# Products of B and C on the two halves of rows, and quarters first: one change to a graph-and-Mamba kernel

## The chip, the cores and the metric

The kernel runs on one core of a Trainium2 chip. The metric is the device time of one execution in microseconds (us). Before the change it is 2470.87 us, the median of 14 runs that lie between 2467.94 and 2473.18.

Engines are named as in the profile: PE is TensorE's matmul, PEld its weight load, DVE is VectorE, ACT is ScalarE, POOL is GpSimd, SP is SyncE. "SPq" is the queue in which SP issues transfers. "L744" is line 744 of the kernel before.

## The reference, cut to what matters

The input x is 64 graphs of 256 nodes with 256 features, all in float32, and adj is one 256x256 matrix of zeros and ones for each graph. There are two layers, each with a mixing part and a part like a feed-forward; every part works on a layernorm of x and is added to x.

```python
x = x + graph_attention(layernorm(x), adj)           # per graph, scores masked by adj
x = x + mamba2_block(layernorm(x))                   # d_state 64, 8 heads of 64, conv of 4, chunk 256
x = x + relational_gnn(layernorm(x), relation=adj)   # adj's entries name the relation
x = x + moe_top1(layernorm(x))                       # 8 experts 256 -> 1024 -> 256, capacity 1.25 T/E
```

In the Mamba2 block, a projection, a causal convolution and silu give xh (8 heads of 64), B and C (64 wide each) for every node. With one chunk per graph, the output is

```python
Y_diag = einsum('bcln,bcsn,bhcls,bcshp->bclhp', Cc, Bc, Lmat, xdt)
```

so each graph needs one 256x256 product of C and B, contracted over only 64 values, of which the causal part (s not after l) is used. It is multiplied by each head's decay (Lmat), and the result multiplies that head's xdt. In the last part each node goes to one of 8 experts; nodes past an expert's capacity are dropped.

## The kernel before, in words

**Prologue.** Weights are loaded and folded (the products of two weight matrices, centred weights) in a pool of its own. Its last lines (L586 to L591) transpose the experts' b1 and write it to a scratch tensor, b1d, from which pass 2 reads; that write is issued by SP. Behind it in SP's queue stand the loads of the first group's adj and x (L805 and L803).

**Pass 1** works on 32 groups of two graphs (512 nodes). A group goes through attention (a graph's nodes on partitions in two tiles), `scan`, `mix`, `relate` and `choose`, and writes its x to x3d and out, and each node's expert and place to a table of slots. Nothing loops at run time. Each operation is registered as a step with an engine, a planned duration, what it reads and what it writes; a planner (`Plan.record`, L180 to L290) then emits all steps of all groups in the order in which its own model says that they can begin. Of the steps on one engine that could begin within 0.05 us of each other, the one of lower rank goes first; the rank is `PACE * group + DUE[k]` for the k-th step of a group, and `LATE[k]` for the steps behind the last group. These tables are numbers in the file. The emitted order is kept, so every engine's queue holds the groups interleaved.

**B and C.** In `scan`, the fifth column block of the convolved projection (`convolved(NCT)`) holds B in rows 0 to 63 and C in rows 64 to 127, with the 512 nodes of the two graphs along the columns (`bm`, L969 to L974). A matmul contracts over rows, so B and C have to stand on the same rows: a transfer (L975) copies rows 64 to 127 of `bm` to rows 0 to 63 of `cm`. The other 64 rows of the two buffers of `cm` are set to zero once, in the prologue (L606 to L610), and the products contract over all 128 rows: B's rows meet C, C's rows meet zeros. `meet` (L1059) makes two products for each graph, 256 wide for the first 128 values of s and 128 wide for the second; DVE multiplies each graph's by the causal mask `trif` (L1064) into `bc`. For each pair of heads DVE multiplies the decays `dm` by `bc` (L1088), and `heads` (L1090) multiplies by xdt. The heads' matmuls use half of the array's columns each (64 outputs), two heads in turns; their form in the profile is 128\*64.

**The end of pass 1.** The lists of blocks are made by a long chain of small DVE steps (`walk`, L635 to L655). A block is up to 512 slots of one expert. Two whole blocks (NEARLY = 2) of the experts run as planned steps within pass 1 (`first_block`, L1379 to L1402), beside the last groups.

**Pass 2** (L1480 to L1622) does the other blocks, in three kinds: quarters (128 slots), halves (256) and wholes (512), in this order. Each kind is a nest of run-time conditions, `experts(i)` within `If(listed > i)`. In this run 4 quarters, 1 half and otherwise wholes are done. For a block, `fetch_slots` (SP) loads the table's rows, `gather` (POOL) computes places and fetches the rows of x3d with one indirect transfer for each 128, `fetch_weights` (SP) loads w1, b1, w2 and b2 (1 MB for each of w1 and w2), `norm` (DVE, L415) and `turned` (PE and ACT, L1545) make the block's normed rows and transpose them, `experts` multiplies by w1 (L1563) and w2 (L1573), and the result is scattered to the output (L427). `experts(i)` begins by issuing the weights of block i+1, the slots and the rows of block i+2, and norms block i+1. The second weight buffer of the quarters is also that of the wholes.

Before the loops, the code issues for all three kinds, in this order: the slots of blocks 0 and 1, the rows of blocks 0 and 1, the weights of block 0, and the norm and transposes of block 0. A small matmul then makes a number (`general`) that says whether the program must run again in a general form; it doesn't here. Tile's scheduler puts in the waits; each engine runs its own instructions in the order of the code.

Of the kernel before, what the change touches and what calls it, by code (L numbers as in the profile page):

```python
# [9 lines left out]
F32 = mybir.dt.float32  # L10
# [4 lines left out]
ALU = mybir.AluOpType  # L15
# [4 lines left out]
P = 128  # L20
# [11 lines left out]
PACE = 4.60  # L32
DUE = [
    -187, -691, -72, 159, -113, -114, -149, 636, 174, 171, 387, 756, -229, -1087, -1172, 20, -351,
    -599, 699, -611, -1484, 249, -770, -710, -1048, 376, -331, 864, -405, 61, -28, 134, 16, -9,
    348, 442, -429, -1102, -42, 703, -223, 113, -607, 108, 990, 202, 295, 646, 26, 263, -92, 233,
    247, -557, -374, -723, 667, 329, -360, -253, -391, -1223, -304, -600, -778, -988, -488, -62,
    -720, -720, -306, -566, -4, 261, -344, 153, -232, -603, -36, -391, 947, 502, -439, -94, -126,
    29, -246, 327, -208, -945, 61, -486, -490, -648, -49, 120, 553, 10, -408, -1120, -935, -301,
    -1702, 164, -515, 586, -50, -355, 132, 744, -80, 96, -1, 160, -115, 422, 133, 217, -609, 128,  # L40
    -1196, 106, -198, -115, -589, -56, 549, -876, -729, 476, -280, -741, -486, -186, -114, 171,
    711, -911, -300, -262, 1079, -444, -107, -98, 127, 135, -372, -12, -97, 504, 638, 342, -669,
    -318, 1, 363, -806, -1604, -646, -790, 276, -140, 264, -165, 370, 251, 14, -435, -518, -133,
    -470, -615, 98, 237, -148, -214, -868, -1044, -884, 125, 722, 505, 627, 310, 101, 280, 264,
    947, 409, -79, 138, -8, -1018, -924, -303, -515, -328, -216, -660, 755, 133, 127, -181, 129,
    -683, -19, 86, -697, 353, 242, -391, 243, -479, -626, 320, 328, 221, -542, -377, 191, 161,
    -181, 223, -433, -295, 139, 127, 151, -181, 152, -496, -30, 178, -458, 330, 615, -10, 301,
    198, -168, 566, 303, -1378, -203, 504, -349, 138, 15, 93, -300, -469, -71, -1080, -905, -382,
    -765, -499, 522, -559, -436, -711, -1062, -307, -489, 705, -263, 262, 48, 538, -87, -172, -7,
    -532, -975, -688, -187, -1308, -570, 302, -1059, -506, 779, 83, -11, 749, -4, 216, 469, 900,  # L50
    -1142, 86,
]
LATE = [
    439, 482, 387, 262, 460, 193, 260, 587, 397, 193, 239, 309, 207, 431, 312, 489, 501, 247, 320,
    397, 398, 341, 500, 377, 575, 532, 367, 505, 283, 139, 276, 464, 345, 243, 455, 107, 575, 200,
    296, 296, 296, 296, 296, 296, 296, 296, 296, 296, 296, 296, 170, 321, 356, 486, 13, 179, 363,
    192, 357, 768, 395, 1857, 2047, 1812, 2046, 1886, 2036, 1982, 2016, 1957, 1976, 1757, 1937,
    1678, 2042, 1873, 2052, 2162, 2018, 2061, 1964, 2122, 1809, 397, 1880, 2090, 446, 466, 2153,
    1801, 208, 1845, 1887, 420, 371, 1753, 2084, 343, 1955, 1982, 469, 302, 1752, 1929, 128, 2080,
    1921, 332, 270, 332, 389, 145, 449, 139, 514, 497, 334, 177, 408, 502, 1660, 1834, 1843, 1988,  # L60
    2202, 2247, 2273, 2186, 2179, 1985, 1853, 1933, 1944, 2220, 1882, 2133, 1815, 2009, 2179,
    2095, 1789, 1828, 563, 1802, 1733, -146, 109, 1792, 2073, 414, 1763, 1943, 143, 509, 2344,
    2010, 508, 2033, 2085, 250, 423, 2196, 2256, 716, 2018, 1585, 411, 176,
]


class Home:

# [219 lines left out]
def gnn_mamba_rgcn_moe(ctx: ExitStack, tc: tile.TileContext, a: dict, out: bass.AP):  # L288
# [1174 lines left out]
    def second_pass(form, pass2):  # L1463
# [136 lines left out]
        for blocks in three:  # L1600
            for i in range(2):
                blocks.fetch_slots(i)
# [68 lines left out]
```

## Time and profile before

| What | Value |
|---|---|
| median of 14 runs | 2470.87 us (2467.94 to 2473.18) |
| the profiled execution's own time | 2472.09 us |
| its span in the profile | 2470.4 us |
| PE busy | 2355.6 us (95%) |
| DVE busy | 1915.2 us (78%) |
| ACT busy | 1634.9 us (66%) |
| POOL busy | 825.9 us (33%) |
| PE's last instruction of pass 1 ends | 1846.65 us |
| last result of pass 1 is sent (L427) | 1852.71 us |
| first matmul of pass 2's first quarter begins | 1874.99 us |
| first matmul of its first whole block begins | 1934.31 us |

The profile comes from one execution; its times run from the span's start. A row of a timeline gives the begin, the length from the first begin to the last end of a run of like instructions, the engine, the line, the operation, the tiles (written <- read), the shapes, the count, and in brackets the idle time of the engine before it with what ended it. In a row of stretches, each engine has its busy time with its number of instructions. L744 is the line of a helper, `product`, that many steps use, so its rows are told apart by their tiles. The times in pass 1 that the prediction uses are from the stretch 800 to 1100 us, which is one of steady work.

### The profile page before, as it was taken

The numbers are of one execution on the slowest core, as the hardware profiler recorded it, in microseconds if no ns is written. First come the engines' busy times: TensorE is split into PE (matmuls) and PEld (weight loads), VectorE is DVE, ScalarE is ACT, GpSimd is POOL, SyncE is SP. The second block draws the span as 40 slices with busy tenths as digits, with TensorE's granted clock in tenths as the row PEclk, the third lists the DMA queues.
The fourth block names the chain that finished last, engine by engine and source line by source line (L and its number), as shares of the span: only waits on it lengthen the run. The fifth ranks groups of instructions, "written<-read, shape, count | busy, mean of one in ns | idle before, by whom it ended". The sixth has DMA issues, their size and how long they took to land.

```text
span 2470.4 us, 35015 instructions
## 1 busy us (share of the span) xinstructions
PE 2355.6 (95%) x11448; PEld 1645.7 (67%) x11451; DVE 1915.2 (78%) x4825; ACT 1634.9 (66%) x3720; POOL 825.9 (33%) x762
## 2 busy tenths in 40 slices
PE   5999999999999999999999999999886999999996
PEld 4567777667767666776766777666655566666664
DVE  4899999999999999999999999999772234444333
ACT  2878888888888888888888888887522232223321
POOL 1122334333342433334333343432524222222221
PEclk8999999999999999999999999999997999999998
DMA  3212222322222322222332222321537333333332
GB/s 116 46 23 54 63 62 66 80 57 55 63 62 65 79 59 55 63 55 72 73 65 55 63 55 72 65 55 40 140 106 255 109 115 123 109 111 130 110 116 61
DMA packets 173527, 198.93 MB, mean 81 GB/s; under 512 B 25448, under 2 KB 157870, under 8 KB 173312
## 3 DMA queue, kind: packets, MB, share of 16 engines
q1 hardware_dynamic: 124816, 135.70, 16.8%
q0 software_dynamic: 46816, 58.88, 13.0%
q8 instruction: 98, 1.61, 0.3%
q10 hardware_dynamic: 1680, 1.79, 0.3%
q14 instruction: 117, 0.96, 0.1%
HBM read 112.47 MB, written 45.45 MB: 64 GB/s over the span
## 4 chain that ended last, share of the span: by engine, by line
issue 33%; DVE 33%; POOL 13%; PE 10%; ACT 8%; DMA 3%; POOLq 0%; SPq 0%; ACTq 0%; DVEq 0%
PE ps L744 8%; DVE y L963 8%; POOL rs L752 5%; POOL out_dram L427 3%; POOL xg L409 3%; DVE gate L946 3%; DVE xh L1105 2%; DVE gate L1108 2%; DVE st L760 2%; DVE dm L1088 2%; DMA xg<-x3d,place 2%; DVE xdt L1078 1%; DVE ev L857 1%; DVE ev L859 1%; DVE bm L973 1%
## 5 line engine op out<-in xcount | busy, mean ns | idle before, releaser
L744 PE MATMUL ps<-xnT,win 128*128 128x512 f32 x1152 | 543.4, 601 | 4.0 <-ACT xnT L786 3.9
L963 DVE SCALAR_TENSOR_TENSOR y<-ps,cw,y 128x510 f32<-128x510 f32 (+2 forms) x480 | 351.0, 738 | 6.1 <-ACT y L956 4.5
L752 POOL TENSOR_TENSOR rs<-ve,mhalf 128x4 f32<-128x4 f32 x96 | 161.2, 1679 | 529.5 <-DVE ve L750 405.7
L1030 ACT ACTIVATE dm<-ps,cs 128x256 f32<-128x256 f32 (+1 forms) x1024 | 332.6, 472 | 5.5 <-PE ps L744 5.5
L744 PEld LDWEIGHTS ps<-xnT,win 128*128 128x128 f32 x1152 | 205.0, 190 | 171.0 <-issue 159.7
L1563 PE MATMUL ps<-xnT,w 128*128 128x512 f32 (+2 forms) x736 | 279.2, 539 | 11.2 <-DVEq L1619 6.1
L1573 PE MATMUL ps<-w,hid 128*128 128x256 f32 x1248 | 276.3, 379 | 0.0
L1573 PEld LDWEIGHTS ps<-w,hid 128*128 128x128 f32 x1248 | 235.3, 190 | 38.7 <-issue 8.6
L744 PE MATMUL ps<-wf,gate 128*128 128x265 f32 x1024 | 252.2, 389 | 0.0
L1563 PEld LDWEIGHTS ps<-xnT,w 128*128 128x128 f32 x736 | 134.1, 197 | 146.0 <-issue 138.0
L1088 DVE TENSOR_TENSOR dm<-dm,bc 128x1536 f32<-128x1536 f32 x128 | 225.7, 1764 | 0.5 <-ACT dm L1036 0.2
L1567 ACT ACTIVATE hid<-ps,b 128x512 f32<-128x512 f32 (+2 forms) x184 | 114.5, 622 | 165.0 <-PE ps L1563 163.1
L744 PEld LDWEIGHTS ps<-wf,gate 128*128 128x128 f32 x1024 | 191.7, 190 | 47.9 <-issue 10.9
L1578 DVE TENSOR_TENSOR yv<-ps,b 128x256 f32<-128x256 f32 x78 | 33.1, 425 | 228.4 <-PE ps L1573 228.3
L1036 ACT ACTIVATE dm<-dm 128x1536 f32<-128x1536 f32 x128 | 198.6, 1554 | 0.0
L1282 POOL DMA_INDIRECT slots<-meta,sl x128 | 127.9, 999 | 200.1 <-DVE sl L1279 149.1
L427 POOL DMA_INDIRECT out_dram<-yf,place x78 | 77.7, 997 | 315.5 <-DVE yf L1586 315.2
L1095 PE MATMUL ps<-dm,xdt 128*64 128x256 f32 x1024 | 167.6, 394 | 2.0 <-DVE dm L1088 1.5
L760 DVE BATCH_NORM_STATS2 st<-x 128x6 f32<-128x256 f32 x384 | 151.6, 413 | 6.8 <-DMA x<-in_x_dram 6.2
L969 ACT ACTIVATE xh<-y 128x512 f32<-128x512 f32 x160 | 101.0, 631 | 75.9 <-DVE y L963 66.4
L1579 ACT ACTIVATE yv<-yv,meta 128x256 f32<-128x256 f32 x78 | 39.7, 509 | 168.1 <-DVE yv L1578 168.1
L744 PE MATMUL ps<-wh,eT 128*128 128x273 f32 x512 | 141.7, 406 | 4.6 <-ACT eT L882 4.6
(314 smaller groups left out, 5011.4 us busy)
## 6 DMA issues: line engine op xcount, KB each, us to landing
w<-in_L_ffn_w_dram SPq DMA_DIRECT2D x52, 1024.0 KB, 5.6
x<-blin POOLq DMA_DIRECT2D x32, 530.0 KB, 6.2
x<-brel POOLq DMA_DIRECT2D x32, 530.0 KB, 6.7
adji<-in_adj_dram SPq DMA_DIRECT2D x32, 512.0 KB, 3.8
x<-in_x_dram SPq DMA_DIRECT2D x32, 512.0 KB, 4.7
x3d<-x SPq DMA_DIRECT2D x32, 512.0 KB, 3.1
out_dram<-x SPq DMA_DIRECT2D x32, 512.0 KB, 4.1
cm<-bm SPq DMA_DIRECT2D x32, 128.0 KB, 2.2
```

What stands on the lines that cost most here:

```text
L427: apart("out", nc.gpsimd.indirect_dma_start(out=outf, out_offset=bass.IndirectOffsetOnAxis(ap=col, axis=0), in_=yf, in_offset=None, bounds ...
L744: nc.tensor.matmul(out_, lhsT=lhsT, rhs=rhs, start=(i == 0), stop=(i == len(pairs) - 1))
L752: s.step(POOL, 1.0, lambda: nc.gpsimd.tensor_tensor(rs(), ve(), mhalf[:, 0:4], ALU.pow), [ve], [rs])
L760: s.step(DVE, 0.34, lambda j=j: nc.vector.bn_stats(sb()[:, j, :], src()[:, j, 0:D]), [(src, j)], [(sb, j)])
L963: nc.vector.scalar_tensor_tensor(y3[:, :, d:], p3[:, :, : N - d], cw[:, c, k : k + 1], y3[:, :, d:], ALU.mult, ALU.add,)
L1030: nc.scalar.activation(dm()[:, q, bi, o : o + n], ps()[:, t0 + N - n : t0 + N], AF.Relu, bias=cs()[:, j, h : h + 1], scale=-1.0,)
L1036: s.step(ACT, 1.38, lambda: nc.scalar.activation(dm(), dm(), AF.Exp, scale=-1.0), [], [dm])
L1088: s.step(DVE, 1.67, lambda dm=dm: nc.vector.tensor_mul(dm(), dm(), bc().unsqueeze(1).to_broadcast([P, 2, 2, N + P])), [bc], [dm])
L1095: nc.tensor.matmul(o, lhsT=xdt()[:, 2 * bi, h * 64 : (h + 1) * 64], rhs=dm()[:, q, bi, 0:N], start=True, stop=False,)
L1282: s.step(POOL, 1.1, lambda j=j: apart("slots", nc.gpsimd.indirect_dma_start(out=slots, out_offset=bass.IndirectOffsetOnAxis(ap=sl()[:, j : ...
L1563: nc.tensor.matmul(ps[:, :n], lhsT=w1[:, k, f * P : (f + 1) * P], rhs=xnT[:, k, :], start=(k == 0), stop=(k == 1),)
L1573: nc.tensor.matmul(ps[:, :D], lhsT=hid[:, f, j * P : (j + 1) * P], rhs=w2[:, f, :], start=(f == 0), stop=(f == NFT - 1),)
```

## The change

Three parts of the code change, and the planner's tables.

1. Two transfers of 64 rows by 256 columns take the place of one of 64 rows by 512: C of the first graph goes to rows 0 to 63 of `cm`, and B of the second graph goes to rows 64 to 127 of `cm`. So the first graph's B (`bm`) and C (`cm`) stand on rows 0 to 63, and the second graph's B (`cm`) and C (`bm`) on rows 64 to 127. The products contract over 64 rows, and the two graphs' products are emitted in turns, as one step with two PSUM tiles: the 256 wide ones of both, then the 128 wide ones of both. Nothing has to be zero any more, so the two memsets go.
2. The write of b1d is issued on POOL's queue in place of SP's.
3. Before pass 2's loops, the slots of block 0 of all kinds are loaded, then, for each kind, the rows of block 0 are gathered and the slots of block 1 loaded; then the weights of block 0 are issued; then only the quarters' block 0 is normed and transposed; then the rows of block 1 of all kinds are gathered. The halves' block 0 is normed and transposed behind the quarters' loop, the wholes' behind the halves' loop, and the matmul for `general` comes behind the quarters' loop.
4. PACE, DUE and LATE hold other numbers. DUE has one entry less, since a group has one step less.

```diff
-PACE = 4.60
+PACE = 8.40
 DUE = [
-    -187, -691, -72, 159, -113, -114, -149, 636, 174, 171, 387, 756, -229, -1087, -1172, 20, -351,
...
+    -365, -564, -24, 226, -42, -270, -235, 680, 329, 203, 365, 828, -156, -954, -1301, -14, -269,
...
 LATE = [
-    439, 482, 387, 262, 460, 193, 260, 587, 397, 193, 239, 309, 207, 431, 312, 489, 501, 247, 320,
...
+    428, 530, 326, 204, 472, 234, 309, 790, 568, 311, 165, 241, 231, 294, 506, 590, 380, 199, 357,
...
-            nc.sync.dma_start(out=b1d.rearrange("e p k -> p e k"), in_=b1t)
+            nc.gpsimd.dma_start(out=b1d.rearrange("e p k -> p e k"), in_=b1t)
...
-        sides = []
-        for i in range(2):
-            side = wts.tile([P, 512], F32, name=f"cm{i}")
-            nc.gpsimd.memset(side[64:], 0.0)
-            sides.append(side)
+        sides = [wts.tile([P, 512], F32, name=f"cm{i}") for i in range(2)]
...
                 if c == NCT:
-                    s.step(SP, 0.1, lambda: nc.sync.dma_start(out=cm()[0:64], in_=bm()[64:P]),
-                           [bm], [cm], late=2.5)
+                    def crossed():
+                        nc.sync.dma_start(out=cm()[0:64, 0:N], in_=bm()[64:P, 0:N])
+                        nc.sync.dma_start(out=cm()[64:P, N:], in_=bm()[0:64, N:])
+
+                    s.step(SP, 0.1, crossed, [bm], [cm], late=2.5)
...
             bc = s.tile("bc", [P, 2, N + P])
+            pss = [s.psum() for _ in range(2)]
+
+            def meet():
+                for o, n, h in ((0, N, 0), (N, P, P)):
+                    for bi, rows, b_, c_ in ((0, slice(0, 64), bm, cm), (1, slice(64, P), cm, bm)):
+                        product(pss[bi]()[:, o : o + n], [(
+                            b_()[rows, bi * N + h : bi * N + h + P],
+                            c_()[rows, bi * N + h : bi * N + h + n])])
+
+            s.step(PE, 0.67, meet, [bm, cm], pss)
             for bi in range(2):
-                ps, t0, t1 = s.psum(), bi * N, bi * N + P
-
-                def meet(ps=ps, t0=t0, t1=t1):
-                    product(ps()[:, 0:N], [(bm()[:, t0 : t0 + P], cm()[:, t0 : t0 + N])])
-                    product(ps()[:, N : N + P], [(bm()[:, t1 : t1 + P], cm()[:, t1 : t1 + P])])
-
-                s.step(PE, 0.67, meet, [bm, cm], [ps])
-                s.step(DVE, 0.48, lambda bi=bi, ps=ps: nc.vector.tensor_mul(
-                    bc()[:, bi, :], ps()[:, : N + P], trif), [ps], [(bc, bi)])
+                s.step(DVE, 0.48, lambda bi=bi: nc.vector.tensor_mul(
+                    bc()[:, bi, :], pss[bi]()[:, : N + P], trif), [pss[bi]], [(bc, bi)])
...
         three = (quarters, halves, wholes)
         for blocks in three:
-            for i in range(2):
-                blocks.fetch_slots(i)
+            blocks.fetch_slots(0)
         for blocks in three:
-            for i in range(2):
-                blocks.gather(i, nc.gpsimd)
+            blocks.gather(0, nc.gpsimd)
+            blocks.fetch_slots(1)
         for blocks in three:
             blocks.fetch_weights(0)
+        quarters.turned(quarters.norm(0), 0)
         for blocks in three:
-            blocks.turned(blocks.norm(0), 0)
-        if form == "fast":
...
-        for blocks in three:
+            blocks.gather(1, nc.gpsimd)
+        for k, blocks in enumerate(three):
             with ExitStack() as nest:
                 for i in range(blocks.most):
                     nest.enter_context(tc.If(listed[blocks.kind] > i))
                     blocks.experts(i)
+            if k < 2:
+                three[k + 1].turned(three[k + 1].norm(0), 0)
+            if k == 0 and form == "fast":
...
```

## The prediction

> **What bounds the kernel now.** I read the page first, then busy time by stretches, then the timelines of the places that the change touches. The page gives the span and TensorE's share; the stretches say where that share means something (columns: length, then busy us and instruction counts of PE, PEld, DVE, ACT, POOL, then the granted clock, DMA share, GB/s).
>
> ```profile
> span 2470.4 us, 35015 instructions
> PE 2355.6 (95%) x11448; PEld 1645.7 (67%) x11451; DVE 1915.2 (78%) x4825; ACT 1634.9 (66%) x3720; POOL 825.9 (33%) x762
> ...
> 800.00:1100.00 300.00, 297.62 (x1579) 208.99 (x1577) 286.74 (x688) 251.22 (x589) 115.19 (x99) 1.00 0.28 64
> ...
> 1830.00:1860.00 30.00, 15.80 (x64) 12.75 (x62) 14.64 (x46) 3.62 (x7) 11.97 (x17) 0.78 0.66 211
> 1860.00:1900.00 40.00, 29.31 (x166) 24.70 (x166) 9.37 (x30) 12.72 (x36) 14.86 (x21) 0.76 0.84 276
> ```
>
> In pass 1 PE is busy 297.6 of 300 us at the full clock, DVE 286.7 (96%). A pair of groups takes 106.3 us (from one store of x3d to the next but one). So a us of PE work removed in pass 1 is nearly a us of time, as long as DVE's 4% (2.2 us a group) keeps up. Between the passes, 1830 to 1900, PE is idle 25 of 70 us: there the order of waits decides, not work.
>
> **1. The products of B and C.** Each group's two products, and the heads' products that already use half arrays:
>
> ```profile
> 999.64 0.81 PE L744 MATMUL ps<-cm,bm 128*128 128x256 f32 x4
> 1000.29 0.38 PE L744 MATMUL ps<-cs_parts,sel 128*128 128x512 bf16 x1
> ...
> 1002.23 1.06 PE L744 MATMUL ps<-wrel,hr 128*128 128x265 f32 x4
> 1003.26 0.66 PE L1095 MATMUL ps<-dm,xdt 128*64 128x256 f32 x4
> 1003.72 0.42 PE L1099 MATMUL ps<-dm,xdt 128*64 128x128 f32 x4
> 1003.93 0.65 PE L1095 MATMUL ps<-dm,xdt 128*64 128x256 f32 x4
> 1004.37 0.44 PE L1099 MATMUL ps<-dm,xdt 128*64 128x128 f32 x4
> 1004.74 0.50 PE L744 MATMUL ps<-wh,eT 128*128 128x273 f32 x1
> ```
>
> One graph's products (a 256 and a 128 wide one, two instructions each) hold PE from 999.64 to 1000.29, 0.65 us; two graphs 1.30 us a group. The heads' visit has the widths of four such graphs, which in turn would take 2.6 us; on the two halves of columns it takes 1.48 us (1003.26 to 1004.74), that is 2 x 0.65 plus 0.18. So halves do run side by side, and entering and leaving the mode costs something: over the 95 visits of this kind, what stands between the ideal end of the instruction before and the first head has a median of 0.10 us, the excess on the way out 0.22. The trace has no pair on halves of **rows**; the nearest row is this one. By it four products take 0.65 + 0.10 + 0.16 (between the 0.11 us on the way out of the short visits of L1005 and 0.22) = 0.91 us instead of 1.30: 0.39 us a group, 32 groups, **12.5 us**. Bounds: fully side by side and free to enter, 0.65 us a group, 21 us; not side by side at all, 1.30 + 0.3 for the mode, a loss of 10 us.
>
> A weight load of 128 columns takes 190 ns, one of 64 columns 135 (rows of L744 and L1095), and the new pair has eight of the long kind where the heads have the short kind. The Trainium skill, "TensorE: Matmul & The Clock Gate", section "LDWEIGHTS (loading the stationary operand)", speaks against the change: a load costs by its columns, 128/1.2 = 107 ns, however few rows it fills. Were loads of both halves one stream, an estimate from that page would be eight loads, 0.86 us, 1.1 with the mode's cost, and the saving only 6 us. "TensorEngine Tiling (Array Packing)", section "Tiling Modes", says the opposite of one stream (tiles load and multiply in parallel) and that a change of mode drains the array; the drain agrees with the 0.10 and 0.22 us here. No run here shows the row halves.
>
> What else comes with it: C and B cross in two transfers of 64 KB instead of one of 128 (2.2 us to landing, planned with 2.5 us to spare; SP issues one more, 0.47 us of a queue that is mostly empty). DVE's two multiplies by tri (0.54 us each) stay, but now both follow the one step. The built program shows them back to back, then the first multiply of dm (1.76 us). Before, only one stood between the last product and dm, and the heads waited on just that chain: products end 1000.29, L1064 at 1000.71, dm at 1001.36, ready 3.1 us later than the product, heads 1003.26. The chain grows by 0.5 us; against it the new order puts one more wh,eT product (0.95 us) before the heads. I cost it at nothing; uncovered it is 0.5 us x 32 = 16 us, which I keep for the range.
>
> **2. The planner's numbers.** PACE, DUE and LATE only rank steps that could begin at once. In the built order of PE the heads are done in 100 visits instead of 111: 11 x 0.3 = **3 us**. PE's remaining stalls in pass 1 are about 1 us a group (a pair's 106.3 us against 101.4 of pure streaming and some 3 of mode visits), so a better order can win at most 32 us and I count none of it; a worse one has no such limit (rival B).
>
> **3. The end of pass 1.** Here the new order differs in a way that can be priced.
>
> ```profile
> 1825.25 0.51 ACT L1396 ACTIVATE y<-y,hide 128x256 f32<-128x256 f32 x1 [13.05 <-DVE y L1394]
> 1829.49 1.22 PE L1388 MATMUL ps<-xh,dm 128*128 128x256 f32 x2 [4.22 <-ACT dm L1379]
> ```
>
> DVE walks the block lists until 1824.7; the first result y waits behind that, ACT's queue waits 13 us for y, and the relus that PE needs stand behind it in ACT's queue: PE idles 4.2 us, then 0.9. In the new order the first y stands before the last five triples of the walk (0.6 us each), and one y instead of two is ahead of the next two relus. So **3 us**, between 0 and the 5.1 that PE idles.
>
> **4. The start.** x, adj and all behind them wait in SP's queue for the write of b1d.
>
> ```profile
> 42.75 0.39 SPq L591 DMA_DIRECT2D b1d<-b1t  x1
> 43.23 0.53 SPq L805 DMA_DIRECT2D adji<-in_adj_dram  x1
> 43.85 3.77 SPq L803 DMA_DIRECT2D x<-in_x_dram  x5
> 49.19 0.66 PE L781 MATMUL ps<-ident,x 128*128 128x128 f32 x2 [6.92 <-DMA x<-in_x_dram]
> ```
>
> On POOL's queue b1d holds up only blank, which has until the first slots are written. In the built program adj then waits for DVE's work of 23 us, and the first x for the fourth wf (42.6) because of the memory it reuses: 1.2 us earlier, with adj no longer ahead of it. **2 us**, bounds 1 and 2.5. The two memsets left out (0.52 us each on POOL) lay under the parameters' loads.
>
> **5. The start of pass 2.** POOL gathers in the order of its queue, and PE's queue has all three kinds' transposes ahead of the first quarter.
>
> ```profile
> 1854.40 1.07 POOL L409 DMA_INDIRECT xg<-x3d,place  x1 [0.28 <-POOL place L406]
> ...
> 1861.03 0.69 PE L1545 MATMUL ps<-ident,xn 128*128 128x128 f32 x2 [14.38 <-DVE xn L415]
> ...
> 1874.99 5.67 PE L1563 MATMUL ps<-xnT,w 128*128 128x128 f32 x32 [0.16 <-issue]
> ...
> 1912.08 8.83 PE L1563 MATMUL ps<-xnT,w 128*128 128x256 f32 x32 [4.11 <-DMA w<-in_L_ffn_w_dram]
> ```
>
> The first quarter's rows land at 1860.5, its weights at 1839.3; it could begin at 1862.7 instead of 1875.0. What is late next is quarter 1's weights: issued 1859.3 and 1862.1 (the buffer is pass 1's before), landed 1874.4 and 1878.5 in a DMA system at 84%. So quarter 1 begins at 1874.5 instead of 1884.6, and 2 and 3, with weights landing every 7 us as the buffers come free, keep that: -10 us. Against it, the halves' transposes now stand after the quarters' loop: DVE gets there at 1911.1, two norms 0.8, transposes and copies 1.1, then the count: PE begins at 1913.3 instead of 1912.1, +1.2. The wholes' four norms (1.4) and eight transposes and two copies (1.3) come after the halves: +2.7 on the 6.05 us that PE already idles at 1934.3. Sum **-6 us**. If the weights came as late as the quarters' start is early, only the +4 would remain; if they come in time, -8.
>
> **Sum.** -12.5 -3 -3 -2 -6 = -26.5 us. The profiled execution took 2472.1 (span 2470.4, 1.7 around it), the median of 14 runs is 2470.9; from the two comes 2445.6 and 2444.4. I say 2445.
>
> **Rivals.**
> A. The halves of rows do not overlap, the change not doing what it says: products 0.2 to 0.3 us a group slower instead of 0.39 faster, +20 us: 2465. For: no row shows it; eight long weight loads. Against: the heads. 0.14.
> B. Slower: at the end of the products DVE is inside a dm multiply (1.76 us) that stands ahead of L1064, as its 96% allows; dm is late and the heads wait 1.76 us in each group: +56, 2501. It turns the sign from 0.83 us a group (26.5/32). For: the chain before had no slack at all. Against: the built order has both multiplies next to each other and more PE work behind them. 0.08.
> C. The new order also takes half of PE's 1 us of stalls a group: -16, 2429. 0.14.
> D. Weights, or the uncovered 0.5 us of chain, eat part: +10 to +16, 2458. 0.14.
> The forecast with its own range, 2437 to 2453: 0.50.
>
> **The numbers.** 2429 to 2466 leaves out B and the edges of A and C. A measurement here can tell about 0.2%, 5 us. Faster by more: forecast, C, D and most of A, 0.88; within: the rest of A and the mild end of B, 0.05; slower: B, 0.07.
>
> **What would show it.** Rows of bm,cm with 64 rows that start within some 30 ns of each other, and the four products in 0.9 us a group; a pair of groups in 105.2 us; L1563 of the first quarter less than 2 us after its transposes, and quarter 1's end set by a DMA of w; the first transposes of x at 47. Wrong if product rows of both halves stand one after the other, if PE before L1095 waits on dm by half a us or more in each group, or if the quarters wait longer for w than they now do for the wholes' rows.

## The result, and the profile after

The changed kernel takes **2501.26 us** (median of 6 runs, 2498.21 to 2501.59) beside 2470.89 of the kernel before (28 runs): ratio 1.012, 95% interval 1.011 to 1.013. The forecast was 2445 with a range to 2466; it is wrong in sign, by 56 us. All times below are from the trace of one execution (2501.3 us) unless a median is named. A "pair" is the time from one store of x3d to the next but one, as the mean over 22 groups from the fifth store on; that is two groups of pass 1. Beside e5 to e7 the kernel before took 2515 us and beside e8 2536, though e5 and e6, run again as e12 beside a kernel before of 2471, kept their own times to 4 us, so for e5 to e8 own times and pairs are compared and not ratios.

The page of the changed kernel:

```profile
span 2499.6 us, 35154 instructions
...
PE 2352.6 (94%) x11437; PEld 1627.5 (65%) x11451; DVE 1934.6 (77%) x4825; ACT 1641.3 (66%) x3720; POOL 835.7 (33%) x761
```

Two of the stretches of the prediction (the second shifted by the 30 us that pass 1 ends later; the columns are the same):

```profile
800.00:1100.00 300.00, 290.63 (x1561) 201.60 (x1563) 284.64 (x668) 248.85 (x583) 118.14 (x98) 1.00 0.29 66
1890.00:1930.00 40.00, 30.73 (x185) 27.62 (x186) 9.23 (x31) 14.04 (x42) 16.54 (x21) 0.88 0.92 315
```

In pass 1 PE was busy 297.6 of 300 us and is now busy 290.6, at the same full clock. It works less and waits more. The pair has grown from 106.28 to 108.25 us, the last store of x3d comes at 1820.65 instead of 1791.13 (+29.5), and what lies behind that is as long as before: so the whole loss is made in the steady part of pass 1.

PE's waits of over 0.15 us between 200 and 1650 us (what waits, for whom; total, times, longest), first the changed kernel:

```profile
PE ps L741 <- ACT hr L1200: 14.9, 13, 1.7
PE ps L741 <- ACT xnT L783: 12.6, 14, 1.0
PE ps L778 <- ACT xn L793: 11.2, 13, 0.9
```

and the kernel before:

```profile
PE ps L744 <- ACT eT L882: 4.6, 13, 0.4
PE ps L744 <- ACT xnT L786: 3.2, 14, 0.2
PE ps L781 <- ACT xn L796: 2.9, 14, 0.2
```

Thirteen or fourteen times is once a pair. Three waits of about 1 us each have taken the place of three of 0.2 to 0.35 us. These are all of that size: none is for a PSUM bank, or for dm ahead of the heads. With the small ones PE idles 3.12 us a pair instead of 0.79, a loss of 2.33 (six pairs of each trace). PE's work, counted from start to start with the idle time taken off, falls only from 105.49 to 105.09.

The products themselves do what was predicted (rows of the timeline, both halves of one group):

```profile
1014.65 0.48 PE L741 MATMUL ps<-cm,bm 64*128 64x256 f32 x1
1014.66 0.48 PE L741 MATMUL ps<-bm,cm 64*128 64x256 f32 x1
...
1015.51 0.39 PE L741 MATMUL ps<-cs_parts,sel 128*128 128x512 bf16 x1
```

The halves begin 10 ns apart, and the next work begins 0.86 us after the first product, where 0.91 was predicted. A pair's products hold PE 1.71 us instead of 2.61.

**Where the new waits come from** can be read in two chains. First xn (the normed x) and xnT (its transpose). DVE multiplies dm, and POOL's power, which makes 1/sqrt of a variance, starts 0.17 us later (all engines, one window):

```profile
1078.29 1.75 DVE L1091 TENSOR_TENSOR dm<-dm,bc 128x1536 f32<-128x1536 f32 x1
1078.46 2.44 POOL L749 TENSOR_TENSOR rs<-ve,mhalf 128x4 f32<-128x4 f32 x1 [1.89 <-DVE ve L747]
1080.94 0.51 ACT L793 ACTIVATE xn<-x,rs 128x256 f32<-128x256 f32 x1 [0.87 <-POOL rs L749]
1082.69 0.73 PE L778 MATMUL ps<-ident,xn 128*128 128x128 f32 x4 [0.86 <-ACT xn L793]
...
1085.41 2.84 PE L741 MATMUL ps<-xnT,win 128*128 128x512 f32 x6 [0.89 <-ACT xnT L783]
```

The power has 4 columns and takes 1.02 to 1.04 us in 27 of its 81 cases between 200 and 1650, and 2.44 to 2.57 in the other 54; these all lie beside a dm multiply, the 27 never. Here it takes 2.44 and ends 0.86 us after the multiply. ACT waits 0.87 for it, PE 0.86 for ACT, and 2 us later 0.89 more for xnT. In the kernel before 41 of 82 are long, by the same division. (The 67 of 94 and 54 of 95 of the expectations count 13 powers of 8 columns in each kernel with them; those take 2.1 to 2.4 us in both.)

But the same place in the kernel before shows that the stretched power is not what is new here:

```profile
1010.68 1.75 DVE L1088 TENSOR_TENSOR dm<-dm,bc 128x1536 f32<-128x1536 f32 x1
1010.74 1.85 POOL L837 TENSOR_TENSOR x<-wh,sd 128x68 f32<-128x68 f32 x1 [0.46 <-ACT wh L834]
1012.55 1.01 POOL L752 TENSOR_TENSOR rs<-ve,mhalf 128x4 f32<-128x4 f32 x1
1014.95 1.17 PE L781 MATMUL ps<-ident,xn 128*128 128x128 f32 x8 [0.21 <-ACT xn L796]
1015.87 0.36 PE L744 MATMUL ps<-adjT,xhi 128*128 128x256 f32 x1
...
1017.58 1.98 PE L744 MATMUL ps<-xnT,win 128*128 128x512 f32 x4 [0.23 <-ACT xnT L786]
```

There the multiply stretches a small POOL step (1.85 us, 0.30 elsewhere) ahead of the power, and the power ends 2.78 us after its input ve is ready; in the changed kernel it ends 2.52 us after. So the result comes no later. What differs is the order of PE and ACT around it: PE's earlier work ends 0.92 us after the power instead of 1.19, ACT makes a wh between the first two xn (0.4 us), and the eight products of adjT (1.1 us) that stood between the transposes of xn and the products with xnT stand elsewhere. The rows are the same at all 13 or 14 waits of each trace, but no run moved these steps, so the reading is not tested.

Second hr, which ACT copies for the products with wrel, and here it is the other way round: POOL's add of squares (xh<-xh) stops DVE's small steps on lg, the scores by which experts are chosen.

```profile
1035.09 1.43 POOL L1116 TENSOR_TENSOR xh<-xh 128x512 f32<-128x512 f32 x1
1035.11 1.50 DVE L1250 TENSOR_TENSOR lg<-lg,lmx 128x64 f32<-128x64 f32 x1
...
1038.74 1.16 DVE L1255 TENSOR_TENSOR lg<-lg,iota_e 128x64 f32<-128x64 f32 x1
...
1041.88 0.63 ACT L966 ACTIVATE xh<-y 128x512 f32<-128x512 f32 x1 [2.98 <-DVE mv L760]
...
1044.01 1.16 PE L741 MATMUL ps<-wrel,hr 128*128 128x265 f32 x4 [0.96 <-ACT hr L1200]
```

The two lg steps take 0.22 us when free (0.14 is planned); in the kernel before they take 0.78 and 0.68, beside adds that began earlier. Here DVE is 2.2 us late, ACT stands 2.98 us for DVE (the profile names mv; the last y, which this step reads, ends just before it), hr (1043.37) is behind that in ACT's queue, and PE waits 0.96 for hr. So in these rows a DVE instruction with two inputs in SBUF and a POOL instruction hold one another up, the later one waiting; the planner's durations know nothing of it. By its own model the new numbers are better (1741 us for pass 1's steps instead of 1748).

### The profile page after: what moved, and what is told of

Same layout as the page of the kernel before. It is cut to its first block, busy times and chain, and to the rows that moved or that the text cites. A ratio compares the mean times of both kernels' runs of the same rounds, so it can differ in the third digit from the quotient of the medians.

```text
span 2499.6 us, 35154 instructions
## 1 busy us (share of the span) xinstructions
PE 2352.6 (94%) x11437; PEld 1627.5 (65%) x11451; DVE 1934.6 (77%) x4825; ACT 1641.3 (66%) x3720; POOL 835.7 (33%) x761
## 4 chain that ended last, share of the span: by engine, by line
issue 30%; DVE 24%; PE 17%; POOL 14%; ACT 10%; DMA 4%; POOLq 0%; SPq 0%; another core or an unknown queue 0%; DVEq 0%; ACTq 0%
PE ps L741 14%; POOL rs L749 6%; DVE y L960 5%; POOL xg L409 3%; POOL out_dram L427 3%; DVE gate L943 3%; ACT xn L793 2%; DVE st L757 2%; DVE ev L856 2%; ACT dm L1036 2%; DMA out_dram<-yf,place 1%; DVE dm L1091 1%; DVE ev L854 1%; ACT wh L831 1%; PE ps L1076 1%
## 5 line engine op out<-in xcount | busy, mean ns | idle before, releaser
L1030 ACT ACTIVATE dm<-ps,cs 128x256 f32<-128x256 f32 (+1 forms) x1024 | 352.5, 508 | 12.4 <-PE ps L741 12.3
L749 POOL TENSOR_TENSOR rs<-ve,mhalf 128x4 f32<-128x4 f32 x96 | 183.7, 1913 | 475.4 <-DVE ve L747 351.0
L1285 POOL DMA_INDIRECT slots<-meta,sl x128 | 138.7, 1084 | 221.4 <-DVE sl L1282 153.6
L427 POOL DMA_INDIRECT out_dram<-yf,place x78 | 77.9, 999 | 320.1 <-DVE yf L1589 319.8
L1116 POOL TENSOR_TENSOR xh<-xh 128x512 f32<-128x512 f32 x64 | 88.0, 1375 | 212.5 <-ACT xh L1113 212.5
```

The lines of the kernel that those rows point to most:

```text
L427: apart("out", nc.gpsimd.indirect_dma_start(out=outf, out_offset=bass.IndirectOffsetOnAxis(ap=col, axis=0), in_=yf, in_offset=None, bounds ...
L749: s.step(POOL, 1.0, lambda: nc.gpsimd.tensor_tensor(rs(), ve(), mhalf[:, 0:4], ALU.pow), [ve], [rs])
L1030: nc.scalar.activation(dm()[:, q, bi, o : o + n], ps()[:, t0 + N - n : t0 + N], AF.Relu, bias=cs()[:, j, h : h + 1], scale=-1.0,)
L1285: s.step(POOL, 1.1, lambda j=j: apart("slots", nc.gpsimd.indirect_dma_start(out=slots, out_offset=bass.IndirectOffsetOnAxis(ap=sl()[:, j : ...
```

## The experiments

The theories, with the names that the expectations use: **O**, the emission order that the new numbers make is what costs, and the code in the old order gains what was forecast; **M**, the joined step of both graphs' products costs it in any order; **W**, orders differ by the waits that they leave, the DVE and POOL exclusion above all, and the planner's time says nothing of them. A "replay" lets each engine run its emitted steps in their order, with durations from the traces and the exclusion.

**e1_old_order.** The changed code, emitted in the order of the kernel before; the joined products stand where the earlier graph's stood.

```diff
+ORDER = [515, 1, 7579, 0, 8697, ...]   # the steps as the kernel before emits them
```

> The kernel after, with all its edits, but its steps of pass 1 are emitted in the order that the kernel before emits them (that order is written into the file as a list); the merged products of a group stand where the earlier of its two products stood. Theory O (the new order of the steps costs the time, the products themselves gain): PE's idle time per pair of groups is again about 0.8 us in place of 3.1, the pair takes about 105.4 us (106.3 before, less 0.9 of products), and the time is 2455, between 2448 and 2465. Rival M (the merged products cost it in any order: one step holds two PSUM banks, two transfers must have crossed before either graph's product may begin): the pair stays at 108 or more, and the time at 2495 to 2510.

2499.16 us, ratio 1.0117 (1.0101 to 1.0132), pair 108.24: M's numbers. O in this simple form has fallen. But the order is not quite the old one: before, one graph's product stood some 16 us ahead of the other's (1037.41 and 1053.36). Joined at the earlier place, two PSUM banks are held where one was. The waits for xn and xnT are the small ones of the kernel before, that for hr is gone, and the largest wait is now for a bank that DVE's y still reads, one that the changed kernel's list doesn't have:

```profile
PE ps L1235 <- DVE y L1454: 13.6, 13, 1.1
```

So here an order that fits one set of steps does not fit another that differs by one.

**e2_not_in_turns.** The four products graph by graph.

```diff
-                for o, n, h in ((0, N, 0), (N, P, P)):
-                    for bi, rows, b_, c_ in (...):
+                for bi, rows, b_, c_ in (...):
+                    for o, n, h in ((0, N, 0), (N, P, P)):
```

> The kernel after, but the four products of a group are not in turns: both of the first graph on rows 0 to 63, then both of the second on rows 64 to 127. Theory O with the products' gain from side by side: the products need 1.3 us a group or somewhat more in place of 0.86, and as PE idles 3.1 us a pair anyway, part of the 0.9 us a pair is hidden: 2501 to 2514. If the halves overlap in any order of emission, nothing changes: 2501 within 3.

2503.47 us, ratio 1.0137 (1.0122 to 1.0153), pair 108.19. The rows of the halves still begin 10 ns apart and alternate, and the four still take 0.86 us: taking turns in the code is not needed. What puts them in turns, the array or something between the code and it, isn't shown.

**e3_full_rows.** The changed kernel's order, with the products of the kernel before (128 rows, one transfer, zeros).

```diff
-                            b_()[rows, bi * N + h : bi * N + h + P],
-                            c_()[rows, bi * N + h : bi * N + h + n])])
+                            bm()[:, bi * N + h : bi * N + h + P],
+                            cm()[:, bi * N + h : bi * N + h + n])])
```

> The kernel after, with its order of steps unchanged, but the products contract over all 128 rows as before (rows 64 to 127 of cm are zero again, C crosses in one transfer). Theory O: PE does 0.9 us more a pair, the waits stay, and the time is 2501 to 2516, not below 2500. Rival M in the form that the two halves and their two transfers disturb the other work: the waits for hr, xn and xnT go, the time falls to 2470 to 2485.

2510.92 us, ratio 1.0165 (1.0151 to 1.0179), pair 109.03. PE's waits for hr, xnT and xn are each the same to 0.5 us over the whole stretch; the products take 1.31 us a group. In this order the half rows are worth 9.7 us and 0.78 us a pair, so they and their second transfer are no part of the loss. The step stays joined here, so this run says nothing of M as stated above.

**e4_old_start.** The changed kernel with the start of pass 2 of the kernel before (the diff's last hunk undone).

> The kernel after, but what comes before pass 2's loops is in the order of the kernel before (all three kinds gathered, normed and transposed first). By the two profiles the first quarter began 12.7 us sooner after the last result of pass 1, but the first whole block began 0.4 us later: so the new start is worth nothing, and this kernel takes 2500, between 2496 and 2504. By the prediction's sum the new start gains 6 us: 2507.

2499.33 us, ratio 1.012 (1.0105 to 1.0136), as expected from the two profiles: the new start gains nothing.

**e5_numbers_port, e6_before_port, e7_plan_only.** PACE, DUE and LATE sought anew: e5 for the changed code and e6 for the code before with a replay, e7 for the changed code by the planner's own time.

```diff
-PACE = 8.40
+PACE = 8.14633   # e5; e6: 14.228, e7: 13.6079; DUE and LATE likewise
```

> The kernel after with other numbers in PACE, DUE and LATE and nothing else changed. They were sought with a replay of the steps that adds to the planner's model what the two traces show and the planner lacks: heads at 1.5 us, the merged products at 0.87, a power on POOL that waits until a two-input multiply on DVE has ended, and two-input steps of DVE between tiles that wait until an addition on POOL has ended. The replay puts a pair of groups at 104.5 us here (planner's own time 1733), at 109.4 for the kernel after (1741) and at 107.3 for the kernel before (1748), where the chip took 108.2 and 106.3. Theory W (the order is set by numbers that know nothing of the waits between POOL and DVE, and the new order meets more of them): the pair takes 104.5 to 105.7 us, PE idles under 1.2 us a pair, and the time is 2420 to 2455, below both kernels. Rival M (the merged products or their transfers cost it in any order): the pair stays near 108, the time above 2480.

> The kernel before with other numbers in PACE, DUE and LATE, sought with the same replay (products 0.65 us a graph), and nothing else changed. The replay puts the pair at 105.3 (planner's own time 1749, about as before). Theory W: 2430 to 2460, and 8 to 20 us above the kernel after with its numbers sought in this way, which is then what the products on halves of rows and the start of pass 2 are worth. If the old numbers were as good as can be for this chip: 2465 to 2475.

> The kernel after with other numbers in PACE, DUE and LATE, sought with the planner's own time as the measure (1722, where the kernel after has 1741 and the kernel with the numbers sought by the replay 1733). The replay puts the pair at 108.2 and the end of pass 1 at 55 us more than that of the kernel with the numbers sought by the replay. Theory W: the best plan on paper is not the best on the chip: 2470 to 2500, at least 30 us above the kernel with the numbers sought by the replay. If the planner's own time were a good guide: the fastest of all, near 2430.

e5 takes 2491.84 us (9 less than the changed kernel; pair 108.7), e6 2479.92 (9 more than the kernel before; pair 106.8), e7 2564.67, 3.8% over 2471. W's times for e5 and e6 did not come; e5's are those that M gave. e7 is slower than W had it. e7's plan is the best on paper, 1722, and the slowest on the chip: its pair is 113.2, and PE waits 37.5 us for da and 23.7 for xn. The planner's time is no guide. In e5 PE waits for xn once a pair, 2.96 us in 10 of 13 cases and 1.7 in the others; ahead of xn's power in POOL's queue stand transfers to the slots, and 52 of those beside dm multiplies took 1.5 to 2.9 us (0.97 when free), which this replay left out. So e5 against e6 does not price the products.

**e8_after_line, e8_before_line.** The powers replaced by a line on DVE, at the same place of the order.

```diff
-            s.step(POOL, 1.0, lambda: nc.gpsimd.tensor_tensor(
-                rs(), ve(), mhalf[:, 0:4], ALU.pow), [ve], [rs])
+            s.step(POOL, 1.0, lambda: nc.vector.tensor_scalar(
+                rs(), ve(), -0.5, 1.5, ALU.mult, ALU.add), [ve], [rs])
```

> The changed kernel in its own emission order, with the powers that make 1/sqrt of a variance (POOL, 3 places) replaced by the line 1.5 - 0.5 v on DVE at the same places of the order. So the output differs; what is read is the period of a pair of groups in pass 1 and the ratio. In the changed kernel's trace 67 of 94 of these powers take over 2 us beside DVE's two-input multiplies, and 27 take 1.0; in the kernel before 54 of 95. Theory W (the new order loses on POOL work that DVE's multiplies stretch, which the planner does not know): a replay of the order with these waits gives 107.6 us a pair with the powers on POOL and 105.2 without, so the measured 108.2 falls by about 2.3 us to 106, time near 2465, ratio to the kernel before 0.998; and the gap to the kernel before with the same edit is well below the present 1.9 us. Rival (the waits come from something else, say the joined step or its PSUM banks): the pair stays within 0.7 us of 108.2, time 2490 to 2505, ratio 1.01.

> The kernel before with the same edit (line on DVE in place of powers on POOL; the output differs). Theory W: by the replay 107.1 falls to 105.4, so the measured 106.3 falls by 1.7 us to 104.6 a pair; time near 2444, ratio 0.989. The gap between the two kernels without the powers is then about 1.3 us by these numbers, and none at all if the replay has the rest right (105.2 against 105.4). Rival: the pair stays within 0.7 us of 106.3, the gap stays at 1.9.

Pairs of 108.0 and 109.4, and 2747.8 and 2768.3 us in all, since pass 2 has other work. In the first the pair stayed, as the rival had it; in the second it grew by 3.2 us, which neither theory had. The edit made waits of its own: the line stands in DVE's queue behind the dm multiply, and PE waits ahead of the heads (2.08 us for the line at 644.88 in the second; 26.2 us in all for dm in the first). In the first, PE's waits for xn and hr are gone and that for xnT is 8.9 us in all instead of 12.6, but the one for dm takes nearly all of it back. The changed code is now the faster by 1.4 a pair, but that doesn't say what the powers cost. Inconclusive.

**e9_after_again, e9_after_short_adds, e13_before_short_adds.** The changed kernel unedited, and both kernels with POOL's adds of squares over 32 columns; nothing else moves.

```diff
-                        sq()[:, c, :], sq()[:, c, :], sq()[:, c - 1, :]), ...
+                        sq()[:, c, 0:32], sq()[:, c, 0:32], sq()[:, c - 1, 0:32]), ...
```

> The changed kernel, not edited, beside the other kernels of this call, because the kernel before took 2515 and 2536 us beside the earlier runs instead of 2471. If the slower surroundings leave pass 1 alone, the pair of groups is 108.2 us again and the ratio is 1.01; if they act on the transfers that pass 1 waits for, they act on both kernels, but not by the same amount, and the ratios of those runs have to be read beside this one.

> The changed kernel in its own emission order with POOL's three adds of squares over 32 of 512 columns (the sums of squares are then wrong, the rest of the work stays). In the changed kernel's trace an add (1.3 us) stands beside DVE's lg steps at 1035.1 and 1038.5: they take 1.50 and 1.16 us where 0.14 is planned, ACT then waits 2.98 us for DVE's mv, hr stands behind that in ACT's queue, and PE waits 0.96 us for hr once a pair. Theory W: without the adds that wait of PE goes, the pair is 0.7 to 1.3 us shorter than the changed kernel's of the same call (108.2 to about 107.2), ratio lower by 0.006. Rival: DVE is late for another reason and the adds are hidden; the pair stays within 0.3 us and PE still waits for hr.

> The kernel before with the same short adds of squares on POOL (32 of 512 columns; the sums of squares are wrong). In the changed kernel they took 1.6 us a pair away (108.2 to 106.6). Theory W: in the order of the kernel before, PE has no wait for hr and idles 0.79 us a pair in all, so the adds are nearly hidden there: the pair falls by 0 to 0.6 us from 106.3, ratio 0.995 to 1.0, and most of what the short adds gave the changed kernel is the price of its order. Rival: the adds cost both orders the same; 104.7 a pair, ratio 0.989.

Unedited: 2500.52 us, ratio 1.0121 (1.0105 to 1.0138), pair 108.33. With short adds the changed kernel takes 2479.6, ratio 1.003 (1.0018 to 1.0041), pair **106.56**, and the wait for hr is gone from its list:

```profile
PE ps L741 <- ACT xnT L783: 12.6, 14, 1.0
PE ps L778 <- ACT xn L793: 11.2, 13, 0.9
```

The kernel before gains 0.43 us a pair from the same edit (105.85; ratio 1.0002, 0.9993 to 1.0012), the changed one 1.69 by its first trace, more than the 0.7 to 1.3 expected. In both, the lg steps fall to 0.2 to 0.3 us. The whole times understate this: with other sums of squares other blocks come out, and pass 2 has 768 matmuls of xnT and w instead of 736. By the last store of x3d the changed kernel is 32.0 us earlier, the kernel before 13.6. So the adds make 18 of the 29.5 us between the two kernels. This was W's number for the kernel before, and the rival's (the same in both) is out. The waits for xn and xnT are untouched by it, and the pairs still differ by 0.7 us.

**e10_after_sought, e10_before_sought.** Numbers sought again for both, for the same time, with indirect transfers in the replay and as a mean over several assumptions.

```diff
-PACE = 8.40
+PACE = -10.5494   # the code before: 14.0993; DUE and LATE likewise
```

> The changed kernel with PACE, DUE and LATE sought anew with a replay of the emitted order that has the waits between DVE and POOL in it, indirect transfers too, and that takes the mean over several assumptions on their lengths. Theory W: order is what the change lost, so numbers that avoid these waits bring pass 1 to 105 to 107 us a pair, below the kernel before (106.3): ratio 0.975 to 0.995. Rival M (the joined step of the products costs the time in any order): pair over 107.5, ratio over 1.0.

> The kernel before with numbers sought in the same way and for the same time. If the products on row halves bring what their rows say (0.45 us a group), this one is slower than the changed kernel with sought numbers by 0.9 us a pair, 14 us in pass 1; the replays say 1781 against 1795. Theory W: pair 106 to 107.5, ratio 0.98 to 1.0. If the joined step costs more than it brings, this one is the faster.

2494.49 and 2497.16 us, ratios 1.0097 (1.008 to 1.0114) and 1.0102 (1.0085 to 1.0119), pairs 107.84 and 108.16. Both are slower than the kernel before; the changed code is ahead by 2.7 us, within the error. My replay misses enough that its orders are no better than those on hand; the 14 us that it gave the products are not confirmed. The first one's numbers are again those that M gave, but the code with two separate steps did no better. From 1130 to 1660 us the changed code runs at 105.9 a pair, below the steady 106.3 of the kernel before and with the joined step, so M does not hold for every order. In the whole of it no power of 4 columns takes over 1.06 us, and the waits for xn and xnT are gone; ahead of 1130 us it loses to a wait for `three` and what follows it, which is shown at the end.

**e11_after_split_dm, e11_after_split_short.** Each dm multiply in two halves; the second with the short adds too.

```diff
-                    dm(), dm(), bc().unsqueeze(1).to_broadcast([P, 2, 2, N + P])), [bc], [dm])
+                    dm()[:, q], dm()[:, q], bc()) for q in range(2)], [bc], [dm])
```

> The changed kernel in its own order, with each of DVE's multiplies of dm by bc (1.75 us) made as two of half the size, one for each of its two heads. The result is the same. In the changed kernel a power on POOL beside such a multiply takes 2.44 us instead of 1.0 and ends 0.9 us after the multiply; ACT's xn waits 0.87 us for it and PE 0.86 us for xn and 0.90 for xnT behind it, once a pair each. Theory W, if the exclusion holds for one instruction at a time: the power gets in between the halves, takes 1.5 to 1.8 us, and PE's waits for xn and xnT (1.76 us a pair) shrink by 0.8 or more; DVE has 8 instructions more a pair, about 0.1 us each. Pair 107.2 to 107.8 instead of 108.2, ratio 1.004 to 1.009. If the halves follow each other so closely that POOL doesn't get in, powers stay at 2.4 us and the pair at 108.2 or more.

> The same split together with POOL's adds of squares over 32 of 512 columns (the sums of squares are wrong): both kinds of DVE and POOL collisions weakened in the changed kernel's own order. The short adds alone gave 106.6 us a pair and ratio 1.003, with PE still waiting 0.86 for xn and 0.90 for xnT. Theory W: 105.4 to 106.2 a pair, below the 106.3 of the kernel before, ratio 0.990 to 0.999. Rival (xn and xnT are late for another reason than the stretched power): 106.6 or more, ratio 1.003 or more.

2492.82 us, ratio 1.0091 (1.0074 to 1.0108), pair 107.88, so a gain of 8 us on the changed kernel, just outside W's range; with short adds 2473.98, ratio 1.0012 (1.0002 to 1.0021), pair 106.22, between W's numbers and the rival's. Of the 81 powers of 4 columns 27 now take 1.68 or 1.77 us and 27 over 2 instead of 54. PE's wait for xn is halved, but that for xnT stays at 0.9, and the power ahead of xn is still long:

```profile
1074.13 2.51 POOL L749 TENSOR_TENSOR rs<-ve,mhalf 128x4 f32<-128x4 f32 x1 [2.17 <-DVE ve L747]
...
1078.43 0.73 PE L778 MATMUL ps<-ident,xn 128*128 128x128 f32 x4 [0.42 <-ACT xn L793]
```

So the split helps other powers, and not the one that it was meant for. That xn waits on a stretched power is what the trace's chain says; no run here took only that away, and it stays open how much of the 1.76 us it makes. The kernel before has the same delay in that chain, and small waits.

**e12_e5_again, e12_e6_again.** e5 and e6, unedited.

> e5 again (the changed kernel with numbers sought by a replay), because the kernel before took 2515 us beside it and 2471 in the other calls. If e5's own time is not touched by that, it is 2492 again and the ratio to 2471 is 1.0085; if it was, it falls with the kernel before and the ratio is 0.991 again.

> e6 again (the kernel before with numbers sought by a replay), for the same reason. Untouched by the surroundings: 2480 again, ratio 1.0036. Touched like the kernel before: ratio 0.986 again, 2436.

2495.25 and 2480.68 us beside 2471.14: ratios 1.01 (1.0083 to 1.0117) and 1.0034 (1.0022 to 1.0045). Neither beats the kernel before. No version that does the whole work was faster than it.

## Why the prediction was wrong

| Step of the prediction | predicted, us | measured, us |
|---|---|---|
| 1 products on row halves | -12.5 | -14.4 (0.90 a pair, 16 pairs); -9.7 by e3 |
| 2 visits of the heads | -3 | -2.7 (0.17 a pair) |
| 2 PE's waits in the new order, "I count none of it" | 0 | +37 (2.33 a pair) |
| other streaming of PE | not named | +11 (0.67 a pair, 0.53 of it at xnT,win) |
| 4 the start | -2 | -1.3 (first group stored at 207.6 instead of 208.9) |
| 3 the end of pass 1 | -3 | -0.3 |
| 5 the start of pass 2 | -6 | -0.9 to the end of the span; +0.4 to the first whole block |

The measured column adds to 28 (with -0.9 for the last row); the spans differ by 29.2. Streaming and waits are from six pairs of each trace, taken times 16.

**Step 2 failed.** The prediction read PE's stalls in the kernel before, saw that little could be won, and costed PE's waits in the new order at zero; the runs show 2.33 us a pair, 37 us, which turns the sign. "A worse one has no such limit" was left to rival B at 0.08. Its reading of the stalls was off as well: it took about 1 us a group from a sum, where the trace has 0.79 us a pair, so a better order could win some 13 us and not 32. It had the built order of each engine, and in the old trace 41 powers of 4 columns at about 1.0 us and 41 at over 2.4, and DVE's bm steps of 0.68 us (18) and of 1.2 to 1.8 (14), and it never asked why one instruction of one size takes two times. With an answer the new order could have been searched for collisions: in it the adds stretch the lg steps to 1.50 and 1.24 us (0.78 and 0.68 in the old order), while the bm steps all take 0.68. The Trainium skill has the rule, in "SBUF — State Buffer", section "Who interferes with whom": a Vector instruction with two SBUF inputs contends with a GpSimd instruction that reads SBUF, and the port pair that they share is an exclusive lock. The traces here agree (the power 2.44 us beside dm, 1.02 to 1.04 in its short cases), and e9 and e13 price one case of it, the adds: 18 us. The rest of the loss, the waits for xn and xnT, is where PE's and ACT's work stands in the new order, by the rows above; that is argued and not tested.

**Rival B's sum was right by luck; its cause was not.** It said 2501, for DVE's dm late at the heads. Behind the products shown above, bc follows the products at 1015.65 and 1016.21, dm at 1016.84, and the heads begin at 1019.36 without a wait: there the 0.5 us by which the chain grew is covered, as step 1 had it.

**Step 1 was right** in mechanism and nearly in size: 0.45 us a group instead of 0.39. Eight weight loads of 180 to 190 ns did not stand in a row; those of the two halves run side by side.

**Steps 3 and 4** had the right sign. The first transposes of x come 2.4 us sooner; of this, 1.3 reach the first store. At the end PE still waits for a relu behind DVE's walk, 3.07 us instead of 4.22 and 0.85:

```profile
46.75 1.94 PE L778 MATMUL ps<-ident,x 128*128 128x128 f32 x8 [4.54 <-DMA x<-in_x_dram]
...
1859.31 16.59 PE L1391 MATMUL ps<-xh,dm 128*128 128x256 f32 x62 [3.07 <-ACT dm L1382]
```

but from the last store of x3d to PE's last instruction of pass 1 only 0.3 us are won.

**Step 5** got the first quarter right and the next late thing wrong (timeline of PE, SP's queue and POOL):

```profile
1892.37 5.56 PE L1566 MATMUL ps<-xnT,w 128*128 128x128 f32 x32 [0.15 <-ACT xnT L1551]
...
1897.14 2.86 SPq L1505 DMA_DIRECT2D meta<-slots  x1
...
1909.55 0.94 POOL L409 DMA_INDIRECT xg<-x3d,place  x1 [5.94 <-DVE place L406]
...
1916.21 0.46 PE L1548 MATMUL ps<-ident,xn 128*128 128x128 f32 x2 [4.10 <-DVE xn L415]
```

The first quarter begins 9.6 us after the last result of pass 1 is sent (L427), 12.7 us sooner than before, and quarter 1 waits 1.21 us for weights, as foreseen. But block 2's slots are fetched by SP only behind the weights, in a DMA system at 92%; they land at 1909.05, the rows follow, and quarter 2 begins 14.0 us after quarter 1 (8.1 before). From the first quarter's first product to the half's it takes 9.7 us longer (46.8 instead of 37.1), from there to the first whole's 3.4 (2.7 predicted). The gain is given back.

What stays open: how the waits for xn and xnT, 1.3 us a pair more than before, divide between the power and the order of PE and ACT; whether the joined step makes good orders harder to find; why the kernel before's own order with its one step less fits so badly (e1's bank wait is one reason, shown, but not all); and what the products bring once an order is made for them on the chip.

## What to carry to other kernels

A new order is a change of its own, and the largest one here: a plan whose durations come from instructions that ran alone has to be read for those that share something, and two durations of one shape in the old trace show where. Cost a reordering by what stands beside each short step whose result another engine needs at once, and by what work the waiting engine still has in hand, not by the idle time that is left to win. And what a change saves on a saturated engine (0.9 us a pair, as read from the rows) arrives only if the queues that feed it keep up to that amount.

## What the runs showed of the hardware

- DVE's steps with two SBUF inputs and POOL's work hold one another up both ways: POOL's power 1.0 us alone, 2.44 to 2.57 beside dm; DVE's lg 0.22 alone, 1.16 to 1.50 beside an add; POOL's issue of an indirect transfer 0.97 alone, up to 1.8 beside dm in the changed kernel and up to 2.9 in e5's repeat.
- A wait of 1.6 us can cost PE more than itself. In e10_after_sought, after such a wait the granted clock fell to half in 5 of 8 cases; in the changed kernel, whose waits from 300 to 1300 us are of at most 1.4 us, it stayed at 1.00 there. Nor is 1.6 us a threshold: in e12_e5_again, from 300 to 1300 us, five waits of 1.71 us left the clock at 1.00, and five of 2.96 to 2.98 brought it to half. The second of e10's eight, by stretches (PE's busy time, then the clock in the third column from the end):

```profile
454.00:456.00 2.00, 0.86 (x4) 0.38 (x2) 2.00 (x5) 1.04 (x3) 0.33 (x1) 1.00 0.00 0
456.00:458.00 2.00, 1.53 (x12) 1.43 (x13) 2.00 (x5) 0.95 (x2) 0.00 (x0) 0.80 0.00 0
458.00:460.00 2.00, 2.00 (x7) 1.42 (x8) 2.00 (x5) 1.59 (x5) 0.82 (x1) 0.50 0.00 0
```

- Matmuls on the two halves of rows run at once, their rows 10 ns apart and four products in 0.86 us, even when the code issues one half's two products and then the other's (e2).
